# Decays of a selective scan one slot ahead, half of them in SBUF, and images stored once for the depthwise convolutions

## The chip, the cores and the metric

The kernel runs on one core of a Trainium2 chip. The metric is the device time of one execution in microseconds (us); the median of several runs is given. A core has five engines that work side by side, each through its own instructions in order: PE (TensorE, matrix products into PSUM), DVE (VectorE), ACT (ScalarE, activation functions), POOL (GpSimd[...]) and SP (SyncE, which here issues all DMAs). An engine that waits for another holds up everything behind it in its own queue.

## The reference

Four layers act on an image batch x of 4 x 128 x 64 x 64 (float32). The change touches layer 0, whose work is, for each of the four images:

```
x_n  = groupnorm(x)                                   # 32 groups
feat = gelu(depthwise3x3(x_n, conv1_w))
ca   = sigmoid(relu(mean(feat) @ ca1_w.T) @ ca2_w.T)
feat = gelu(depthwise3x3(feat * ca, conv2_w))
score of each pixel from feat and from the variance of x_n over channels
order of the 256 patches of 4 x 4 pixels = argsort(-mean score)
tokens = x_n in that order + pe, layernorm            # 4096 x 128
xm, z  = tokens @ in_proj_w.T                         # 256 + 256 channels
xc     = silu(causal conv1d(xm));  dt, B, C from xc @ x_proj_w.T
h_t = exp(dt_t * A) * h_(t-1) + dt_t * B_t * xc_t     # 256 channels x 16 states
y_t = sum over states of h_t * C_t;   out = ((y + D * xc) * silu(z)) @ out_proj_w.T
x = x + out, put back in the old order of pixels
```

Layer 1 adds a dense 3x3 convolution, layer 2 an attention and a feed-forward part, layer 3 a linear attention and a feed-forward part. They are not touched.

## The kernel before

**Stages.** Layers 0 and 1 are one function, `layers01`. Image 0 is prepared alone ("the opening", `in_order(0)`, to about 280 us). Then `scan` runs over the four images in turn, 8 chunks of 512 tokens each, 32 chunks in all. Beside the scan of image b the preparation of image b + 1 is carried out (`in_order`); beside the last scan, the end of images 2, 0 and 1 (put back, groupnorm, 3x3 convolution). The end of image 3 runs alone.

**The scan.** 16 states times 256 channels are 32 rows of 128 partitions. A chunk has 8 groups g (two states each), a group has four rows q, and a slot handles two of them, so a group takes an even slot (i = 0) and an odd slot (i = 1), and a chunk takes 16 slots. Per group, DVE makes `hs` = dtx * B for all four rows (line 900; B comes from PE in PSUM, `b_ps`, one buffer). Per slot, ACT makes two decays exp(a * dt) of 128 x 512 (line 907) in `psex`, a PSUM pool with two buffers; DVE runs two scans (line 911) with a decay and a row of `hs`; POOL copies the last column into `carry` (line 914) and multiplies both rows by C (line 915). PE sums the products over states into `y_ps`. `hs` has three buffers. C is loaded by SP as a broadcast (`c_sb`, three buffers).

**The order of the work** is written out by hand: inside `manual_schedule` each engine executes in the order of emission. A slot emits, in this order: `hs` (even slots), two decays, `K.flush()` (the delayed work: evacuations, activations and sums that earlier slots put off with `later`), two scans, the two POOL instructions, PE's sums of the group before (odd slots), the loading of C (even slots), one step each of `leave` (the chunk before), `enter` (the next chunk) and the work beside, and at last PE's `b_ps` of the next group (even slots). A decay waits until the scan that used its buffer has run, that is, the scan of the slot before.

**The next chunk.** `enter(n + 1)` makes xc, B, C, dt and dtx of the next chunk on PE, ACT, DVE and POOL; SP copies dt and dtx to both halves of the partitions (`dt2`, `dtx2`, two buffers each). Three of POOL's 128 x 1024 instructions per chunk are from here, a fourth (`yt` * `sz`) from `leave`.

**The depthwise convolutions.** PE takes the taps over ky and 32 channels as contraction: the operand `under` has 96 partitions (3 ky x 32 channels) by 4 groups of channels. SBUF rows of an image are 66 wide with their border. So SP stores the image to DRAM (`image_d`) three times, once for each ky, in two halves, 12 DMAs of 32 partitions each per half (line 443), and for each of 8 pieces of 8 rows `gather` loads 96 x 4 x 528 values in one DMA (line 453, two buffers). `first` and `second` are the convolutions; the stores of the normalized image are emitted when it is filled, the stores of the first result (`fp`) behind its fifth and eighth piece.

**Small parts.** `sort` makes a comparison matrix `before` (line 581) per half of the patches, each time anew. `put_back` makes `perm_inv0/1` in buffers of their own. `Common` makes `same4` and `same16` with their intermediate tiles in a pool that stays.

Of the kernel before, what the change touches and what calls it, by code (L numbers as in the profile page):

```python
# [30 lines left out]
class Common:  # L31
# [3 lines left out]
    def __init__(self, tc, pool):  # L35
        self.slot = 0
        self.late, self.count, self.live, self.held, self.banks = [], 0, set(), set(), 8
        nc = self.nc = tc.nc
        self.tc = tc
        self.pool = pool  # L40

        def const(name, shape, value):
            t = pool.tile(shape, F32, name=name)
            nc.vector.memset(t, value)
            return t

# [21 lines left out]
        self.same4 = self.same_block("same4", 2)  # L68
        self.same16 = self.same_block("same16", 4)
        self.group_mean = pool.tile([P, P], F32, name="group_mean")  # L70
        nc.vector.tensor_scalar(self.group_mean, self.same4, 0.25, None, ALU.mult)

    def shifted(self, name, src, n, ops):

        nc = self.nc
        ti = self.pool.tile([P, n], I32, name=name + "_i")
        nc.vector.tensor_scalar(ti, src, *ops)
        tf = self.pool.tile([P, n], F32, name=name)
# [3 lines left out]
    def same_block(self, name, shift):  # L82
        nc = self.nc
        r = self.shifted(name + "_r", self.row_i, 1, (shift, None, ALU.arith_shift_right))
        c = self.shifted(name + "_c", self.col_i[:, 0:P], P, (shift, None, ALU.arith_shift_right))
        t = self.pool.tile([P, P], F32, name=name)
# [183 lines left out]
def layers01(K, xd, dpool, w, w1):  # L270
# [9 lines left out]
    with ExitStack() as ctx:  # L280
# [44 lines left out]
        image_d = [dpool.tile([4, 96, HW * (HW + 2)], F32, name=f"image_d{i}") for i in range(2)]  # L325
# [52 lines left out]
        ones256 = K.ones[:, 0:1].to_broadcast([P, 256])  # L378

# [43 lines left out]
        def in_order(b, made, work, psum):  # L423
# [13 lines left out]
            def stored(img, i, half):  # L437


                n = HW // 2 * (HW + 2)  # L440
                for g in range(4):
                    for ky in range(3):
                        nc.sync.dma_start(
                            out=image_d[i][g, 32 * ky : 32 * ky + 32, n * half : n * half + n],
                            in_=img[32 * g : 32 * g + 32, HW // 2 * half + ky : HW // 2 * (half + 1) + ky, :].rearrange(
                                "p y x -> p (y x)"
                            ),
                        )

            def gather(i, c):  # L450
                n = 8 * (HW + 2)
                t = unders[c] = work.tile([96, 4, n], F32, name="under", bufs=2)
                nc.sync.dma_start(out=t, in_=image_d[i][:, :, n * c : n * c + n].rearrange("g q f -> q g f"))
# [113 lines left out]
            def sort():  # L567
# [6 lines left out]
                for h in range(2):  # L574
# [5 lines left out]
                    before = small.tile([P, 256], F32, name="before")  # L580
                    nc.vector.scalar_tensor_tensor(before, K.col, K.row[:, h : h + 1], ones256, ALU.is_gt, ALU.mult)
                    eq = small.tile([P, 256], F32, name="eq", tag="rank_eq")
                    nc.vector.scalar_tensor_tensor(eq, sm, cl, before, ALU.is_equal, ALU.mult)
# [137 lines left out]
        def scan(seqs, others, work, psum, psbc, psex, psy):  # L721
# [158 lines left out]

            for _ in enter(0):
                K.flush()
            K.flush()
            bb, cs = spread_b(0, 0), spread_c(0, 0)
            past, leaving, coming = None, iter(()), iter(())
            for n, (b, c) in enumerate(chunks):
# [8 lines left out]
                dt2, dtx2 = entered[n][2:]  # L895
                more = n + 1 < len(chunks)
                coming = enter(n + 1) if more else iter(())
                for g in range(NG):
                    hs = work.tile([P, NQ, CH], F32, name="hs", bufs=3)
                    nc.vector.tensor_tensor(hs, dtx2, bb.unsqueeze(1).to_broadcast([P, NQ, CH]), ALU.mult)  # L900
                    for i in range(2):
                        slot = 2 * g + i
                        two = slice(2 * i, 2 * i + 2)
                        decays = []
                        for q in (2 * i, 2 * i + 1):
                            ex = psex.tile([P, CH], F32, name="decay")
                            nc.scalar.activation(ex, dt2[:, q, :], AF.Exp, scale=a_neg[:, q, g : g + 1])  # L907
                            decays.append(ex)
# [45 lines left out]
        def put_back(xb, om, rank, prep, psum):  # L954
# [4 lines left out]
            for h in range(2):  # L959
                pi = small.tile([P, 256], F32, name=f"perm_inv{h}")  # L960
# [1172 lines left out]
```

## Time and profile before

| | |
|---|---|
| runs, median of 3 | 10019.67 us (10018.24 to 10020.51) |
| profiled execution, its own time | 10014.33 us |
| its span, first to last instruction | 10012.5 us |
| busy in the span: PE, DVE, ACT, POOL | 8755.8, 7222.2, 7414.1, 4804.1 us |
| scan, first to last scan instruction | 280.6 to 2733.4 us |
| busy in it: PE, DVE, ACT, POOL | 2030.9, 2081.3, 1519.5, 1656.2 us |
| scans (line 911), 1024 | 1245.8 us, 1266 ns each |
| decays (line 907), 1024 | 693.0 us, 689 ns each |
| POOL's products (line 915), 512 | 1207.5 us, 2358 ns each |

Lines of the profile name the engine, the operation and output <- inputs, then shapes and how often; in brackets or behind a bar stands the idle time before the instruction and what ended it. In the windows each row gives a stretch in us from the span's start, its length, the busy time of PE, of PE's weight loads, of DVE, ACT and POOL, the share of the PE clock that was granted, the share of the DMA engines and GB/s. A row of the waits says which engine's instruction waited for what: us in total, times, longest. "SPq" is the queue that issues DMAs.

### The profile page before, as it was taken

How to read it: one execution, taken by the hardware profiler on the slowest of the kernel's cores; microseconds unless marked ns; L12 is line 12 of the kernel's file. 1: busy time of each engine (PE TensorE's matmuls, PEld its weight loads, DVE VectorE, ACT ScalarE, POOL GpSimd, SP SyncE). 2: the span in 40 equal slices, each digit the busy share in tenths (PEclk: the TensorE clock that was granted, in tenths of full speed). 3: DMA queues.
4: the chain of work that ended last, by engine and by line, in shares of the span. 5: the costliest groups of instructions: out<-in, count | busy, mean ns of one | idle time of the engine just before them, and what ended most of it. 6: DMA issues, size and time to landing. Idle time of an engine off the chain costs nothing.

```text
span 10012.5 us, 187862 instructions
## 1 busy us (share of the span) xinstructions
PE 8755.8 (87%) x74074; PEld 3353.2 (33%) x74074; DVE 7222.2 (72%) x7883; ACT 7414.1 (74%) x10669; POOL 4804.1 (48%) x3175
## 2 busy tenths in 40 slices
PE   5687888889859999979999979999979999967767
PEld 1122222235433333333333333333333333323433
DVE  1779797998738888848888858888758888743463
ACT  2666766654439999969999969999969999941531
POOL 0567586775525555545555545555545555420000
PEclk9787887889979999989999989999989999978888
DMA  5634536222221211141211141211141111133004
GB/s 127 150 88 101 134 79 152 69 73 81 74 70 37 41 39 39 30 115 38 39 39 39 29 115 39 39 38 39 29 115 39 38 39 39 33 100 118 2 18 152
DMA packets 578291, 669.38 MB, mean 67 GB/s; under 512 B 113592, under 2 KB 369664, under 8 KB 570240
## 3 DMA queue, kind: packets, MB, share of 16 engines
q1 hardware_dynamic: 577408, 657.36, 27.1%
q8 instruction: 584, 9.57, 0.4%
q14 instruction: 299, 2.45, 0.1%
HBM read 446.84 MB, written 143.13 MB: 59 GB/s over the span
## 4 chain that ended last, share of the span: by engine, by line
PE 45%; DVE 4%; DMA 2%; ACT 2%; POOL 1%; issue 1%; SPq 1%; DVEq 0%; POOLq 0%; ACTq 0%
PE ctx_ps L91 20%; PE acc_ps L91 10%; PE score L91 8%; PE ln_xc L91 1%; DMA w<-in_L_ffn_weight 1%; PE ln_var L91 1%; PE hid_ps L91 1%; PE kv L91 1%; PE tok_t L1829 0%; PE ln_var L121 0%; PE pool L91 0%; PE ans_ps L91 0%; DVE ctx L1468 0%; PE o_ps L91 0%; SPq L1210 0%
## 5 line engine op out<-in xcount | busy, mean ns | idle before, releaser
L1534 ACT ACTIVATE ex<-score 128x1024 f32<-128x1024 f32 x5120 | 4927.9, 1037 | 176.0 <-PE score L91 90.2
L91 PE MATMUL ctx_ps<-ex,qt 128*32 128x512 f32 x20480 | 2736.5, 606 | 19.8 <-DVE ctx L1468 19.8
L1483 POOL TENSOR_TENSOR folded<-ex 128x1024 f32<-128x1024 f32 x512 | 1224.2, 2391 | 2124.0 <-ACT ex L1534 1866.1
L1540 DVE STREAM_TRANSPOSE turned<-ex 128x1024 f32<-128x1024 f32 x1536 | 1885.9, 1228 | 351.5 <-ACT ex L1534 279.1
L1516 DVE STREAM_TRANSPOSE turned<-ex 128x1024 f32<-128x1024 f32 x1532 | 1843.0, 1203 | 0.0
L91 PE MATMUL acc_ps<-turned,turned_v 128*32 128x256 f32 x24576 | 1769.4, 379 | 3.0 <-DVE turned L1546 3.0
L911 DVE TENSOR_TENSOR_SCAN hs<-decay,carry,hs 128x512 f32<-128x512 f32 x1024 | 1245.8, 1266 | 248.2 <-ACT decay L907 234.9
L91 PE MATMUL score<-queries,keys 32*128 32x512 f32 x10240 | 1333.6, 497 | 64.4 <-POOL queries L1218 35.8
L91 PEld LDWEIGHTS acc_ps<-turned,turned_v 128*32 128x32 f32 x24576 | 800.8, 110 | 1476.5 <-issue 1327.2
L915 POOL TENSOR_TENSOR hs<-hs,c_sb 128x1024 f32<-128x1024 f32 x512 | 1207.5, 2358 | 108.9 <-DMA c_sb<-c_d 66.5
L907 ACT ACTIVATE decay<-dt,a_neg 128x512 f32<-128x512 f32 x1024 | 693.0, 689 | 662.5 <-DVE hs L911 653.0
L91 PEld LDWEIGHTS score<-queries,keys 32*128 32x128 f32 x10240 | 512.1, 182 | 1160.4 <-ACT ex L1534 801.8
L1346 POOL TENSOR_TENSOR turned_v<-v,quarter 128x1024 f32<-128x1024 f32 x256 | 612.5, 2393 | 266.3 <-PE acc_ps L91 221.8
L91 PE MATMUL y_ps<-hs,pair 128*64 128x512 f32 x2048 | 664.0, 776 | 27.0 <-POOL hs L915 26.9
L1484 POOL TENSOR_TENSOR quarters<-folded 128x512 f32<-128x512 f32 x512 | 658.0, 1285 | 40.1
L91 PEld LDWEIGHTS ctx_ps<-ex,qt 128*32 128x32 f32 x20480 | 406.5, 108 | 655.4 <-issue 599.3
L900 DVE TENSOR_TENSOR hs<-dtx,b_ps 128x2048 f32<-128x2048 f32 x256 | 580.5, 2267 | 55.1 <-PE b_ps L91 29.8
L91 PE MATMUL b_ps<-dbc,state 32*64 32x512 f32 x1024 | 339.6, 745 | 224.5 <-DVE hs L900 224.4
L1534 ACT ACTIVATION_READ_ACCUMULATOR ex<-score 128x1 f32 x2048 | 437.7, 214 | 0.0
L914 POOL COPY carry<-hs 128x2 f32<-128x2 f32 x512 | 98.1, 192 | 700.1 <-DVE hs L911 673.9
L1468 DVE COPY ctx<-ctx_ps 128x512 f32<-128x512 f32 x256 | 176.9, 691 | 329.2 <-PE ctx_ps L91 323.5
L91 PE MATMUL conv<-under,deep 96*32 96x512 f32 x1536 | 217.9, 708 | 136.6 <-DMA under<-image_d 128.3
(371 smaller groups left out, 9156.9 us busy)
## 6 DMA issues: line engine op xcount, KB each, us to landing
c_sb<-c_d SPq DMA_DIRECT2D x512, 128.0 KB
queries<-head_d SPq DMA_DIRECT2D x1024, 64.0 KB
keys<-head_d SPq DMA_DIRECT2D x1024, 64.0 KB
under<-image_d SPq DMA_DIRECT2D x64, 792.0 KB
dt<-dt SPq DMA_DIRECT2D x128, 256.0 KB
dtx<-dtx SPq DMA_DIRECT2D x128, 256.0 KB
v<-value_d SPq DMA_DIRECT2D x1024, 32.0 KB
w<-in_L_ffn_weight SPq DMA_DIRECT2D x32, 1024.0 KB
```

What stands on the lines that cost most here:

```text
L91: self.nc.tensor.matmul(out, lhsT, rhs, start=start, stop=stop)
L900: nc.vector.tensor_tensor(hs, dtx2, bb.unsqueeze(1).to_broadcast([P, NQ, CH]), ALU.mult)
L907: nc.scalar.activation(ex, dt2[:, q, :], AF.Exp, scale=a_neg[:, q, g : g + 1])
L911: nc.vector.tensor_tensor_scan(hs[:, q, :], decays[q - 2 * i], hs[:, q, :], carry[:, g, q : q + 1], ALU.mult, ALU.add)
L915: nc.gpsimd.tensor_tensor(hs[:, two, :], hs[:, two, :], cs.unsqueeze(1).to_broadcast([P, 2, CH]), ALU.mult)
L1346: nc.gpsimd.tensor_tensor(t, v.unsqueeze(2).to_broadcast([P, 4 * BT, 4, HD]), quarter.unsqueeze(1).to_broadcast([P, 4 * BT, 4, HD]), ALU.mult,
L1468: nc.vector.tensor_copy(u, cps)
L1483: nc.gpsimd.tensor_tensor(hs, exs[:, :, 0], exs[:, :, 1], ALU.add)
L1484: nc.gpsimd.tensor_tensor(qs, hs[:, :, 0 : CH // 2], hs[:, :, CH // 2 :], ALU.add)
L1516: nc.vector.transpose(*upright)
L1534: nc.scalar.activation(ex, sps[p], AF.Exp, scale=scale, accum_out=sums[:, t : t + 1] if summed else None)
L1540: nc.vector.transpose(*upright)
```

## The change

- **Decays**: a function `decay(m)` makes the two decays of slot m. The first slot's are made ahead of the loop; each slot then emits the decays of the slot after it, ahead of its own delayed work, and its scans take those made a slot earlier. Those of even slots stay in the two PSUM buffers; those of odd slots go into two SBUF buffers (`decay_b`).
- **Images**: `image_d` has one copy of the image with its border, 128 partitions by 66 x 66. It is stored in four quarters of rows, one DMA each, as soon as the rows are there. `gather` loads a piece with three DMAs, one for each ky, from rows shifted by ky.
- **Small parts**: `before` is made once for each half (`befores`), with an instruction that reads one tensor; `perm_inv0/1` take the buffers of `beats0/1`; the intermediate tiles of `same4` and `same16`, and `same4` itself, go into a pool that is given back.

```
+        with tc.tile_pool(name="temporary", bufs=1) as tmp:
+            self.same4 = self.same_block("same4", 2, tmp, tmp)
+            self.same16 = self.same_block("same16", 4, tmp, pool)
...
-        image_d = [dpool.tile([4, 96, HW * (HW + 2)], F32, name=f"image_d{i}") for i in range(2)]
+        image_d = [dpool.tile([P, (HW + 2) * (HW + 2)], F32, name=f"image_d{i}") for i in range(2)]
...
+        befores = [small.tile([P, 256], F32, name=f"before{h}", bufs=1) for h in range(2)]
+        for h in range(2):
+            nc.vector.tensor_scalar(befores[h], K.col, K.row[:, h : h + 1], None, ALU.is_gt)
...
-            def stored(img, i, half):
-                n = HW // 2 * (HW + 2)
-                for g in range(4):
-                    for ky in range(3):
-                        nc.sync.dma_start(
-                            out=image_d[i][g, 32 * ky : 32 * ky + 32, n * half : n * half + n],
-                            in_=img[32 * g : 32 * g + 32, HW // 2 * half + ky : HW // 2 * (half + 1) + ky, :].rearrange(
-                                "p y x -> p (y x)"
-                            ),
-                        )
+            def stored(img, i, q):
+                lo, hi = 16 * q + 1 if q else 0, 16 * q + 17 if q < 3 else HW + 2
+                nc.sync.dma_start(
+                    out=image_d[i][:, lo * (HW + 2) : hi * (HW + 2)], in_=img[:, lo:hi].rearrange("p y x -> p (y x)")
+                )
             def gather(i, c):
                 n = 8 * (HW + 2)
                 t = unders[c] = work.tile([96, 4, n], F32, name="under", bufs=2)
-                nc.sync.dma_start(out=t, in_=image_d[i][:, :, n * c : n * c + n].rearrange("g q f -> q g f"))
+                for ky in range(3):
+                    at = (8 * c + ky) * (HW + 2)
+                    nc.sync.dma_start(
+                        out=t[32 * ky : 32 * ky + 32],
+                        in_=image_d[i][:, at : at + n].rearrange("(g q) f -> q g f", q=32),
+                    )
...
-                if c == 6:
-                    stored(xp, 0, 0)
+                if c in (3, 5, 7):
+                    stored(xp, 0, c // 2 - 1)
...
-            stored(xp, 0, 1)
+            stored(xp, 0, 3)
             def first_stored(c):
-                if c in (4, 7):
-                    stored(fp, 1, c // 5)
+                if c % 2:
+                    stored(fp, 1, c // 2)
...
-                    before = small.tile([P, 256], F32, name="before")
-                    nc.vector.scalar_tensor_tensor(before, K.col, K.row[:, h : h + 1], ones256, ALU.is_gt, ALU.mult)
-                    nc.vector.scalar_tensor_tensor(eq, sm, cl, before, ALU.is_equal, ALU.mult)
+                    nc.vector.scalar_tensor_tensor(eq, sm, cl, befores[h], ALU.is_equal, ALU.mult)
...
+            def decay(m):
+                n, g, i = m // SLOTS, m % SLOTS // 2, m % 2
+                out = []
+                for q in (2 * i, 2 * i + 1):
+                    ex = work.tile([P, CH], F32, name="decay_b") if i else psex.tile([P, CH], F32, name="decay")
+                    nc.scalar.activation(ex, entered[n][2][:, q, :], AF.Exp, scale=a_neg[:, q, g : g + 1])
+                    out.append(ex)
+                return out
...
+            coming_decays = decay(0)
...
-                        decays = []
-                        for q in (2 * i, 2 * i + 1):
-                            ex = psex.tile([P, CH], F32, name="decay")
-                            nc.scalar.activation(ex, dt2[:, q, :], AF.Exp, scale=a_neg[:, q, g : g + 1])
-                            decays.append(ex)
+                        decays = coming_decays
+                        if slot + 1 < SLOTS or more:
+                            coming_decays = decay(SLOTS * n + slot + 1)
                         K.flush()
...
-                pi = small.tile([P, 256], F32, name=f"perm_inv{h}")
+                pi = small.tile([P, 256], F32, name=f"perm_inv{h}", tag=f"beats{h}")
```

More of the change, by code (lines that the diff above doesn't have):

```diff
@@ L66, in __init__, with shifted, same_block @@
         nc.vector.tensor_scalar(self.row[:, 1:2], self.row[:, 0:1], 128.0, None, ALU.add)
[L68 to L73, printed above, removed]
+        with tc.tile_pool(name="temporary", bufs=1) as tmp:
+            self.same4 = self.same_block("same4", 2, tmp, tmp)
+            self.same16 = self.same_block("same16", 4, tmp, pool)
+            self.group_mean = pool.tile([P, P], F32, name="group_mean")
+            nc.vector.tensor_scalar(self.group_mean, self.same4, 0.25, None, ALU.mult)
+    def shifted(self, name, src, n, ops, pool=None):
         nc = self.nc
-        ti = self.pool.tile([P, n], I32, name=name + "_i")
+        pool = pool or self.pool
+        ti = pool.tile([P, n], I32, name=name + "_i")
         nc.vector.tensor_scalar(ti, src, *ops)
-        tf = self.pool.tile([P, n], F32, name=name)
+        tf = pool.tile([P, n], F32, name=name)
         nc.vector.tensor_copy(tf, ti)
         return tf
-    def same_block(self, name, shift):
+    def same_block(self, name, shift, tmp, pool):
         nc = self.nc
-        r = self.shifted(name + "_r", self.row_i, 1, (shift, None, ALU.arith_shift_right))
-        c = self.shifted(name + "_c", self.col_i[:, 0:P], P, (shift, None, ALU.arith_shift_right))
-        t = self.pool.tile([P, P], F32, name=name)
+        r = self.shifted(name + "_r", self.row_i, 1, (shift, None, ALU.arith_shift_right), tmp)
+        c = self.shifted(name + "_c", self.col_i[:, 0:P], P, (shift, None, ALU.arith_shift_right), tmp)
+        t = pool.tile([P, P], F32, name=name)
         nc.vector.tensor_scalar(t, c, r, None, ALU.is_equal)
@@ L894, in scan @@
                         begin, until, pace = 8, NCH * SLOTS, (NB - 1) * TURNS_END / (NCH * SLOTS - 8)
-                dt2, dtx2 = entered[n][2:]
+                dtx2 = entered[n][3]
                 more = n + 1 < len(chunks)
```

## The prediction

> **What bounds the kernel now.** I read the page first (the 40 slices), then the windows view by chunk of the scan, then the waits of that stretch, then the timeline in three places. The program is the layers in a row; the diff touches layers 0 and 1 only, the first 2880 us of 10012.5, and there two stages: the opening (image 0 prepared alone, to 280 us) and the scan (280 to 2733 us, 32 chunks of 16 slots). Windows of the first eight chunks (from scan to scan; columns are PE, PEld, DVE, ACT, POOL):
>
> ```profile
> 280.60:345.30 64.70, 48.28 (x122) 12.38 (x122) 63.25 (x56) 41.75 (x55) 44.15 (x37) 0.72 0.35 90
> 345.30:419.50 74.20, 56.34 (x192) 14.75 (x196) 59.92 (x45) 48.31 (x64) 52.62 (x43) 0.82 0.87 192
> 419.50:494.50 75.00, 64.17 (x270) 17.19 (x262) 60.14 (x46) 57.19 (x76) 45.20 (x34) 0.82 0.74 173
> 494.50:600.00 105.50, 84.11 (x367) 22.50 (x366) 64.24 (x51) 73.05 (x90) 54.28 (x39) 0.85 0.53 123
> 600.00:687.30 87.30, 70.94 (x222) 20.57 (x226) 78.34 (x71) 51.66 (x79) 61.95 (x49) 0.75 0.28 70
> 687.30:757.60 70.30, 62.67 (x246) 28.20 (x245) 65.34 (x55) 49.95 (x65) 62.66 (x50) 0.93 0.27 64
> 757.60:819.80 62.20, 47.65 (x138) 13.09 (x134) 59.39 (x45) 39.21 (x52) 46.60 (x34) 0.81 0.30 73
> ```
>
> DVE is the bound: 59.4 of 62.2 us in a light chunk. It idles only in the chunks with the two depthwise convolutions (14, 15 and 41 us in the second, third and fourth). The waits of the scan say for whom:
>
> ```profile
> DVE hs L911 <- ACT decay L907: 234.9, 106, 18.1
> PE conv L91 <- DMA under<-image_d: 62.0, 11, 11.4
> ```
>
> That is 78, 69 and 68 us in the first three sequences, 19 in the last (which waits for the 3x3 convolution on PE). The 18.1 us one is at 497: ACT sits in its queue before the Gelu of a convolution whose gathered rows have not landed. So both halves of the change aim at a real loss.
>
> The opening, from the timeline:
>
> ```profile
> 35.45 27.89 SPq L443 DMA_DIRECT2D image_d<-xp  x24
> 63.39 27.61 SPq L453 DMA_DIRECT2D under<-image_d  x6
> 72.37 7.95 PE L91 MATMUL conv<-under,deep 96*32 96x512 f32 x48 [40.63 <-DMA under<-image_d]
> 126.55 13.68 SPq L443 DMA_DIRECT2D image_d<-fp  x12
> ```
>
> The image is complete at 38 us and the first convolution runs at 72: 24 stores and the first gather lie between.
>
> **What the change may collide with.** DVE and POOL around 630 us:
>
> ```profile
> 629.81 2.34 POOL L915 TENSOR_TENSOR hs<-hs,c_sb 128x1024 f32<-128x1024 f32 x1
> 629.92 2.51 DVE L581 SCALAR_TENSOR_TENSOR before<-col,row,ones 128x256 f32<-128x256 f32 x1
> 632.11 1.37 POOL L612 TENSOR_TENSOR pe<-pe,xp 128x512 f32<-128x512 f32 x1
> 632.47 1.29 DVE L583 SCALAR_TENSOR_TENSOR eq<-sm,cl,before 128x256 f32<-128x256 f32 x1
> 633.79 0.48 DVE L585 SCALAR_TENSOR_TENSOR beats<-sm,cl,eq 128x256 f32<-128x256 f32 x1
> ```
>
> A DVE instruction of 0.48 us that reads two tensors in SBUF takes 2.51 beside a POOL product: it ends 0.28 us after the product does. The POOL sum behind it then takes 1.37 (1.17 elsewhere), and the next DVE instruction waits for that one. They take turns, whole instructions at a time, and a DVE instruction already waiting goes ahead of POOL's next. The four scans at 757.57 (4.81 us together), with decays in PSUM, run at full speed across a POOL product.
>
> [...] The old stores are 32 partitions each: 6.49 MB in about 30 us, 217 GB/s; the trace has no store of 128 partitions to compare. [...]
>
> **The change, part by part.**
>
> *Decays one slot ahead.* The same 1024 activations, 0.69 us each on ACT. They wait for the same scans as before (those of the slot before the current one) and stand before the same delayed work, so nothing on ACT moves back; but the scans that need them come a slot later. A lateness of ACT up to one slot (2.4 us of two scans, plus 2.2 for the product in every second slot) is covered. The copies of dt by SP are needed at slot 15 rather than 16; they are issued near slot 10, so at no price. Table loads (155 before L907) alternate as before. Cover gone, a late decay costs what it costs today.
>
> *Half of the decays in SBUF.* In odd slots both inputs of the scans are now in SBUF, 512 scans, and each must have the port to itself. Per pair of slots today: product L900 2.2 + four scans 4.8 = 7.0 on DVE, beside 2 x 2.55 = 5.1 on POOL (carry and product). After: POOL's product of the even slot starts only when the odd scans have ended (its carry, 0.25 us behind the even scans, finds the port taken). From that end POOL needs 2.25 + 0.25 + 2.35 = 4.85; DVE needs 2.2 + 2.4 = 4.6 to reach the next odd scan and waits 0.25; then scan 1.1, carry 0.1, scan 1.1. Period 7.15: the pairs alone cost almost nothing. But the port is now full, so what else POOL does adds up instead of running beside: three sums and products for the next chunk and the gate, 4 x 2.36 alone, 2.2 each on the port, 8.8 per chunk; and DVE's own two SBUF instructions, 1.7. A light chunk: 8 x 7.15 + 8.8 + 1.7 + 0.8 for the rest = 68.5, against 62.2.
>
> So, chunk by chunk (first sequence, before to after): 64.7 to 71 (statistics add 5.4 of DVE, partly beside POOL); 74.2 to 69.5; 75.0 to 70; 105.5 to 86 (PE has 84 us there, some at a low clock, and becomes the bound); 87.3 to 85 (POOL 62 + scans 19 + other DVE pairs 6, less 2 of overlap); 70.3 to 80.5 (twelve more POOL products, L676, 10); 62.2 to 68.5; 63.2 to 69. Sum -3. The other two sequences are 5 us shorter today, mostly in the fourth chunk: +2 each. The last: four chunks bound by PE unchanged, four +4 each, less 11 of decay waits: +5. Scan: +6.
>
> Behind a delayed POOL stand its products, for which PE's y_ps waits in order (up to 2 us later where PE has room); behind a delayed DVE stands PE's b_ps. Neither is late in the chunks that PE bounds.
>
> *Stores and gathers.* 192 stores of 264 KB go, 32 of about 540 KB from 128 partitions come: 2.2 MB instead of 6.5 per image. At the old 217 GB/s 10 us, at the rate of the xb loads (four of 512 KB from 19.6 to about 28 us) below 8; I take 8, beginning at 35. 64 gathers become 192 with the same bytes; in the opening a gather takes 5.7 us from its free buffer to the next convolution. Three pieces of 32 partitions: 0 to 1 us more, I take 0.5. SP issues 224 instead of 256. First convolution at 49 (today 72); pairs of convolutions every 10.4 + 0.5, last at about 95 (today 126, with an 11.7 us wait behind the stores of fp); the second eight at 5.8 us each, set by PE and ACT, end at 146 (today 184). Opening -37, between -28 and -42. In the scan shorter stores also free SP for c_sb; counted in the fourth chunk's gain.
>
> *The rest.* Eight L581 (2.5 us each in the scan) become two at the start; in the fifth chunk's sum. perm_inv in the buffers of beats: their readers ended a sequence ago, no price. Temporaries: none.
>
> Sum: -37 + 6 = -31. On the profiled execution's 10014.3 (span 10012.5 and 1.8 around it) 9983; the median of the runs is 5.3 higher, so 9989, say **9990**.
>
> **Rivals.**
> - *B, the scan isn't held by the port.* Then the middle gaps go and nothing comes: about -10, -10, -19, -7 and -2 per sequence, -140 for three, -10, opening -37: 9833. For it: no scan with two SBUF inputs is in the trace; against it: every other such instruction was held.
> - *C, slower: POOL's product slips between the two odd scans.* POOL then has nothing left during L900 and the even scans: 4.65 + 1.2 + 2.5 + 1.1 = 9.4 per pair of slots, +2.3. In all chunks that PE doesn't bound, about +55 per sequence, +30 in the last, less 37: 10190. It decides early: 14 of 256 pairs eat the -31, and 22 give +20. Against it: at 632.1 the waiting DVE went first.
> - *D, the middle chunks give half.* The port or PE's queue (b_ps, y_ps behind a late product) takes the place of ACT: +17 per sequence: 10040.
> - That the decays don't come ahead can't be: they are emitted there in the fixed order.
>
> **Numbers.** Forecast 0.50 (its own range 9945 to 10040), B 0.08, C 0.17, D 0.25. 0.2%, 20 us, is about what a measurement can tell from no change. Faster: 0.6 of the forecast, B, a tenth of D: 0.41. Same: 0.35 of the forecast, 0.4 of D: 0.27. Slower 0.32. The range leaves out B and most of C: 9890 to 10110.
>
> **What would show it.** Odd slots' scans (decay_b) at 1.5 us or more on average with PSUM ones at 1.2; light chunks near 68 us; POOL's carry and products longer; the wait on decays below 60 us; first convolution near 49 us, scan from about 243. Wrong if odd scans stay at 1.2 (B), or take over 2 (C), or if the fourth chunk stays above 95 (D).

## The result and the profile after

The changed kernel takes **10188.2 us** (10173.0 to 10191.4, 4 runs), beside 10020.1 for the kernel before: a ratio of 1.016, 95% interval 1.0143 to 1.0178. The profiled execution has a span of 10186.1 us, 173.6 above that of before. Its parts:

| | before | after | difference | forecast |
|---|---|---|---|---|
| opening, to the first scan | 280.6 | 230.4 | -50.2 | -37 |
| scan, 32 chunks | 2452.8 | 2657.5 | +204.7 | +6 |
| all that follows, not touched | 7279.1 | 7298.2 | +19.1 | 0 |

So the loss lies in the scan. In what follows, "the port" is a name for what the odd scans and POOL's instructions take in turn, whole instructions at a time. The prediction inferred it from other instructions; for the scans the profile after shows it: each of the 176 odd ones that took over 1.4 us ends 1.04 to 1.09 us after an instruction of POOL has ended, while those with their decay in PSUM took 1.27 us on average beside POOL's instructions of over 1 us and 1.26 away from them. What it is in the hardware, no run shows. Windows of the first chunk and of the fourth to the seventh (the fourth to the sixth stood at 105.5, 87.3 and 70.3 us before):

```profile
230.40:306.00 75.60, 50.45 (x122) 13.13 (x122) 74.44 (x56) 42.06 (x55) 55.05 (x38) 0.69 0.30 85
...
458.60:550.20 91.60, 79.59 (x367) 21.82 (x366) 78.03 (x52) 72.86 (x90) 57.37 (x38) 0.91 0.52 118
550.20:647.80 97.60, 73.76 (x212) 20.62 (x214) 89.69 (x70) 52.87 (x79) 66.38 (x49) 0.71 0.25 63
647.80:738.20 90.40, 71.07 (x254) 30.68 (x252) 82.11 (x55) 50.23 (x65) 72.05 (x50) 0.84 0.20 50
738.20:808.80 70.60, 50.94 (x138) 13.52 (x134) 68.32 (x45) 39.66 (x52) 61.21 (x34) 0.73 0.26 64
```

DVE has about as many instructions as before and is busy for 9 to 17 us more per chunk (65.3 to 82.1 in the sixth); POOL is busier too. Of the first seven only the fourth chunk, where DVE had waited for decays, is shorter. The groups name the instructions that grew, with the two lines of before first:

```profile
L911 DVE TENSOR_TENSOR_SCAN hs<-decay,carry,hs 128x512 f32<-128x512 f32 x1024 | 1245.8, 1266 | 248.2 <-ACT decay L907 234.9 <-ACT dtx L793 0.5
L915 POOL TENSOR_TENSOR hs<-hs,c_sb 128x1024 f32<-128x1024 f32 x512 | 1207.5, 2358 | 108.9 <-DMA c_sb<-c_d 66.5 <-PE conv L91 2.7 <-PE y_ps L91 1.1
...
L923 DVE TENSOR_TENSOR_SCAN hs<-decay_b,carry,hs 128x512 f32<-128x512 f32 x512 | 912.5, 1822 | 7.9 <-ACT decay_b L890 7.9
L923 DVE TENSOR_TENSOR_SCAN hs<-decay,carry,hs 128x512 f32<-128x512 f32 x512 | 628.2, 1268 | 16.6 <-ACT spreads L656 0.5
L927 POOL TENSOR_TENSOR hs<-hs,c_sb 128x1024 f32<-128x1024 f32 x512 | 1349.2, 2635 | 46.4 <-DMA c_sb<-c_d 3.8 <-PE b_ps L93 1.6 <-POOL carry L926 0.6
```

A scan whose decay is in PSUM takes 1268 ns, as before (1266); one whose decay is in SBUF takes 1822, and POOL's products rise from 2358 to 2635. By position in the group: of the 256 first odd scans 52 take over 3 us, of the second 65; the even ones never exceed 1.4. Each scan that was held starts in earnest when some instruction of POOL ends, 1.04 to 1.09 us before its own end. Put down to that instruction, of the 288 us that the odd scans took above 1.26 us each, 207 lie behind POOL's product with C, 72 behind its sums and products for the next chunk (line 132), and 8 behind the rest. The waits, of the scan stage:

```profile
DVE hs L923 <- ACT decay_b L890: 7.9, 6, 2.3
...
DVE hs L914 <- PE b_ps L93: 91.7, 45, 5.7
...
PE y_ps L93 <- POOL hs L927: 89.3, 43, 4.7
```

The wait for decays is gone (234.9 before). In its place DVE waits for `b_ps` (29.8 before), and PE for POOL's products (25 before).

The clock that was granted to PE in the scan fell as well, from 0.84 to 0.80 (the last column but two):

```profile
280.60:2733.40 2452.80, 2030.89 (x7183) 728.20 (x7184) 2081.34 (x1732) 1519.51 (x2037) 1656.16 (x1257) 0.84 0.41 100
...
230.40:2887.90 2657.50, 2118.01 (x7186) 744.95 (x7186) 2401.14 (x1726) 1527.80 (x2035) 1975.91 (x1257) 0.80 0.33 83
```

A slower PE does not explain the loss: DVE's busy time grew by 320 us, more than the scan did, and DVE stood idle for less time, 256 us instead of 371. Whether the clock has a share in the longer waits for `b_ps` is not shown.

### The profile page after: what moved, and what is told of

Read it like the earlier page. It is cut to its first block, busy times and chain, and to the rows that moved or that the text cites. A ratio compares the mean times of both kernels' runs of the same rounds, so it can differ in the third digit from the quotient of the medians.

```text
span 10186.1 us, 187935 instructions
## 1 busy us (share of the span) xinstructions
PE 8846.9 (87%) x74074; PEld 3376.0 (33%) x74074; DVE 7542.1 (74%) x7877; ACT 7420.1 (73%) x10669; POOL 5124.0 (50%) x3175
## 5 line engine op out<-in xcount | busy, mean ns | idle before, releaser
L927 POOL TENSOR_TENSOR hs<-hs,c_sb 128x1024 f32<-128x1024 f32 x512 | 1349.2, 2635 | 46.4 <-DMA c_sb<-c_d 3.8
L923 DVE TENSOR_TENSOR_SCAN hs<-decay_b,carry,hs 128x512 f32<-128x512 f32 x512 | 912.5, 1822 | 7.9 <-ACT decay_b L890 7.9
L93 PE MATMUL y_ps<-hs,pair 128*64 128x512 f32 x2048 | 701.2, 811 | 92.7 <-POOL hs L927 92.0
L890 ACT ACTIVATE decay<-dt,a_neg 128x512 f32<-128x512 f32 x512 | 347.3, 690 | 520.2 <-DVE hs L923 515.1
L914 DVE TENSOR_TENSOR hs<-dtx,b_ps 128x2048 f32<-128x2048 f32 x256 | 580.1, 2266 | 121.9 <-PE b_ps L93 91.7
L923 DVE TENSOR_TENSOR_SCAN hs<-decay,carry,hs 128x512 f32<-128x512 f32 x512 | 628.2, 1268 | 16.6 <-ACT spreads L656 0.5
L93 PE MATMUL b_ps<-dbc,state 32*64 32x512 f32 x1024 | 361.0, 789 | 276.9 <-DVE hs L914 276.8
L890 ACT ACTIVATE decay_b<-dt,a_neg 128x512 f32<-128x512 f32 x512 | 355.8, 718 | 323.8 <-DVE hs L923 315.1
L926 POOL COPY carry<-hs 128x2 f32<-128x2 f32 x512 | 223.8, 437 | 647.5 <-DVE hs L923 621.9
```

What stands on the lines that cost most here:

```text
L93: self.nc.tensor.matmul(out, lhsT, rhs, start=start, stop=stop)
L890: nc.scalar.activation(ex, entered[n][2][:, q, :], AF.Exp, scale=a_neg[:, q, g : g + 1])
L923: nc.vector.tensor_tensor_scan(hs[:, q, :], decays[q - 2 * i], hs[:, q, :], carry[:, g, q : q + 1], ALU.mult, ALU.add)
L926: nc.gpsimd.tensor_copy(carry[:, g, two].unsqueeze(2), hs[:, two, CH - 1 : CH])
L927: nc.gpsimd.tensor_tensor(hs[:, two, :], hs[:, two, :], cs.unsqueeze(1).to_broadcast([P, 2, CH]), ALU.mult)
```

## The experiments

Twelve kernels were run, in four batches with the kernel before in each. Its medians there, and beside the changed kernel, are 10020 to 10031, so less than about 10 us between two batches is not read. In the table, "ratio" is to the kernel before with its 95% interval, and "excess" what the scans with a decay in SBUF took in all above 1.26 us each, from the trace.

| kernel | us | ratio | scan stage us | scans with SBUF decay, ns | excess us |
|---|---|---|---|---|---|
| changed kernel | 10188.2 | 1.016 (1.0143 to 1.0178) | 2657.5 | 1822 | 288 |
| e_images | 9934.3 | 0.9913 (0.9899 to 0.9928) | 2408.4 | none | |
| e_decays | 10273.5 | 1.0253 (1.0236 to 1.027) | 2708.4 | 1829 | 291 |
| e_best | 9924.2 | 0.9898 (0.9883 to 0.9913) | 2410.7 | none | |
| e_own_slot | 10201.6 | 1.0179 (1.0163 to 1.0194) | 2674.3 | 1828 | 291 |
| e_short_best | 9841.6 | 0.9816 (0.9801 to 0.9831) | 2324.6 | none | |
| e_short_after | 9823.8 | 0.9795 (0.9779 to 0.9812) | 2303.2 | 1344 | 43 |
| e_one_product | 10124.5 | 1.0098 (1.0083 to 1.0113) | 2603.2 | 1629 | 189 |
| e_one_of_four | 10077.9 | 1.0048 (1.0031 to 1.0064) | 2552.7 | 2078 | 209 |
| e_even_half | 10084.1 | 1.0054 (1.0039 to 1.0069) | 2558.5 | 1677 | 213 |
| e_short_roots | 10158.2 | 1.013 (1.0115 to 1.0145) | 2648.2 | 1820 | 287 |
| e_flush_after | 10129.2 | 1.0103 (1.0086 to 1.012) | 2600.9 | 1648 | 198 |
| e_flush_best | 9925.7 | 0.9903 (0.9888 to 0.9917) | 2405.4 | none | |

### Which half of the change costs the time

`e_images` is the kernel before with the new stores and gathers alone; `e_decays` is the change without them, small parts included.

```
 e_images, against before
+        image_d = [dpool.tile([P, (HW + 2) * (HW + 2)], F32, name=f"image_d{i}") for i in range(2)]
...
+            def stored(img, i, q):
...
+                for ky in range(3):
...
 e_decays, against the changed kernel: the same lines taken back
```

> The kernel before with the stores and gathers of the change alone; decays as before, all in PSUM. Theory (the shared port of DVE and POOL costs the time, the images pay): opening 50 us shorter as in the changed kernel, waits of the scans on decays down from 235 us to 120 to 160 because the rows land earlier, time 9900 to 9940. Rival (the gathers in three pieces of 32 partitions cost the time): opening shorter but the scan longer than 2453 us, time above 10020.

> The change without its images: stores and gathers as before, decays one slot ahead and half of them in SBUF, small parts as in the change. Theory (port): opening 280 us, the scan about 2660 to 2690, odd scans 1.7 to 1.9 us on average, time 10230 to 10270. Rival (transfers): not slower than before, 10000 to 10030.

Measured: 9934.3 and 10273.5. The images gain 91 us on their own runs of before (10025.6), the decays lose 248; together they lose 157, where the whole change lost 168, so the two hardly touch each other. `e_decays` lies just outside what was expected (10230 to 10270, scan 2660 to 2690). In the profiled executions of `e_images` and of before, 78 us apart, the opening is 47 us shorter and the scan 44; what follows took 13 longer. The wait for decays, in the scan of `e_images`:

```profile
DVE hs L911 <- ACT decay L907: 184.1, 105, 7.2
```

So 51 of the 234.9 us went without any change to a decay, fewer than expected (120 to 160 us were to be left). PE's wait for the gathered rows fell from 62.0 to 11.4 us; ACT held up behind convolutions whose rows were late, as the prediction read it at 497 us, fits this. The fourth chunk falls from 105.5 to 89.1 by the images alone.

### Looking ahead, or the place of the decays

`e_own_slot` is the changed kernel with every decay made in its own slot again, those of odd slots still in SBUF. `e_best` has the change without its decays (all in PSUM, in their own slot) and without the pool for the temporaries of `same4` and `same16`, which are used once at the start.

```
 e_own_slot, against the changed kernel
-                        decays = coming_decays
-                        if slot + 1 < SLOTS or more:
-                            coming_decays = decay(SLOTS * n + slot + 1)
+                        decays = []
+                        for q in (2 * i, 2 * i + 1):
+                            ex = work.tile([P, CH], F32, name="decay_b") if i else psex.tile([P, CH], F32, name="decay")
+                            nc.scalar.activation(ex, dt2[:, q, :], AF.Exp, scale=a_neg[:, q, g : g + 1])
+                            decays.append(ex)
 e_best, against e_own_slot
...
-                            ex = work.tile([P, CH], F32, name="decay_b") if i else psex.tile([P, CH], F32, name="decay")
+                            ex = psex.tile([P, CH], F32, name="decay")
```

> The changed kernel with every decay made in its own slot again, as before; odd slots' decays stay in SBUF. Theory (port): the port's cost stays and the waits on decays come back in part, so at least as slow as the changed kernel: 10190 to 10260, odd scans 1.6 us or more. Rival (making decays ahead delays the other work on ACT and through it PE and DVE): clearly faster than the changed kernel, below 10080.

> The change without its decays: images stored once, the two masks made once, perm_inv in the buffers of beats; all decays in PSUM in their own slot. Theory (port): a little below the images alone, since eight DVE instructions that read two tensors in SBUF go: 5 to 15 us less. Rival: the same within 5 us, since the fifth chunk is bound by something else.

Measured: 10201.6 and 9924.2. Putting the odd decays into SBUF costs 277 us. Making them a slot ahead brings 13 (10201.6 to 10188.2), which the intervals don't tell from nothing. `e_best` is also the version that beats both kernels: 104 us below its own runs of the kernel before (10028.2). It is 10 us below `e_images`, as expected by number, but not for the reason expected: its opening and scan are as long (234.0 and 2410.7 us, against 233.8 and 2408.4), so nothing is seen there of the eight instructions saved.

The account of DVE in the scan stage, `e_best` to the changed kernel, by the durations of its instructions: 1024 scans, 1294.3 to 1581.9, +288; its other instructions apart from `hs`, 314.3 to 350.2, +36; idle, 332.5 to 256.3, -76. That is +248 (the stage grew by 246.7). The idle time that looking ahead could take was small, because of what came next: between `e_own_slot` and the changed kernel the wait for decays goes from 157 to 8, but the wait for `b_ps` from 29 to 92, that for the convolutions from 38 to 49, and that for ACT's part of dt comes to 32.

### Whether POOL's product is the partner

The same two kernels with POOL's product (line 927) cut to 2 of its 512 columns per row, which leaves out nearly all of the multiplication by C; all instructions and waits remain.

```
-                            hs[:, two, :], hs[:, two, :], cs.unsqueeze(1).to_broadcast([P, 2, CH]), ALU.mult
+                            hs[:, two, 0:2], hs[:, two, 0:2], cs[:, 0:2].unsqueeze(1).to_broadcast([P, 2, 2]), ALU.mult
```

> The change without its decays, and POOL's product with C shortened from 512 columns to 2 (the rest of the states isn't multiplied by C): POOL hardly holds the port. Reference for the next run: DVE still bounds the light chunks at about 60 us, time about 20 to 60 us below the same kernel with full products.

> The changed kernel with the same shortened product (the rest of the states isn't multiplied by C). Theory (port): odd scans back at 1.26 us on average or little more, and the decays one slot ahead now gain: 20 to 80 us below the run with shortened products and the old decays. Rival (decays ahead or SBUF itself cost): as slow against that run as the changed kernel is against its like, 150 us or more.

Measured: 9841.6 and 9823.8. The first lies 83 us below `e_best`, more than the 20 to 60 expected, so full products cost the version without SBUF decays something too. With the product all but gone, the change's decays no longer cost 264 us but gain 18, a little less than the 20 to 80 expected. The group of odd scans in `e_short_after`:

```profile
L923 DVE TENSOR_TENSOR_SCAN hs<-decay_b,carry,hs 128x512 f32<-128x512 f32 x512 | 667.7, 1344 | 7.1 <-ACT decay_b L890 7.1
```

1344 ns: a scan with both inputs in SBUF is not slow by itself; it is slow beside POOL's long instructions. Of its 512 scans 23 are still held, all of them behind POOL's other instructions of 128 x 1024, and these hold back 43 us. The wait for decays that looking ahead was to remove is, in `e_short_best`:

```profile
DVE hs L912 <- ACT decay L908: 165.4, 98, 5.8
```

It falls to 7, but DVE's idle time in the scan falls by only 66 us (288 to 222), since it then waits for `b_ps` (25 to 81) and ACT's part of dt (3 to 27). The 43 us of held scans take back most of the 66: the scan is 21 us shorter.

### Where the product gets in

The timeline of the changed kernel shows two patterns. In the first, of a light chunk, the odd scans follow the even ones at once:

```profile
748.78 2.43 DVE L923 TENSOR_TENSOR_SCAN hs<-decay_b,carry,hs 128x512 f32<-128x512 f32 x2
...
748.92 1.09 POOL L926 COPY carry<-hs 128x2 f32<-128x2 f32 x1 [1.21 <-DVE hs L923]
750.09 3.27 POOL L927 TENSOR_TENSOR hs<-hs,c_sb 128x1024 f32<-128x1024 f32 x1
```

This is the pattern of the forecast: the carry finds the port taken (1.09 us for 0.18 of work), and the product waits for the second odd scan (3.27 for 2.36); DVE loses nothing. In the second pattern, of the sixth chunk, something stands between:

```profile
708.25 0.66 DVE L708 COPY perm_s<-perm_t 128x512 f32<-128x512 f32 x1
...
708.39 0.19 POOL L926 COPY carry<-hs 128x2 f32<-128x2 f32 x1 [0.20 <-DVE hs L923]
708.65 2.36 POOL L927 TENSOR_TENSOR hs<-hs,c_sb 128x1024 f32<-128x1024 f32 x1
708.83 6.49 DVE L923 TENSOR_TENSOR_SCAN hs<-decay_b,carry,hs 128x512 f32<-128x512 f32 x2
710.98 3.26 POOL L132 TENSOR_TENSOR dtx<-dt,xc 128x1024 f32<-128x1024 f32 x1
```

A copy out of PSUM, put off by an earlier slot and carried out by `K.flush()` between the even and the odd scans, is not held by POOL: the 24 of the 32 copies of this line that ran beside a long instruction of POOL took 0.67 us on average, the other 8 0.69. During its 0.66 us POOL's carry goes through, and its product, next in line, has the port 0.2 us ahead of the odd scan. That scan waits to the product's end at 711.0; then comes one scan, then POOL's next instruction, which was waiting too, then the second scan: 6.49 us for two scans of 2.4. In 114 of the 256 groups DVE has work between the even and the odd scans; there the odd pair lost 1.74 us on average (198 us in all), in the other 142 groups 0.63 (90 us). The trace also tells which product held a scan. In the 114 groups it is mostly the product of the even slot just before, as in the second pattern (146 us of the 198). In the 142 that product accounts for 0.7 us; there 53 us lie behind the product of the odd slot of the group before, with which POOL is late, and 30 behind the work for the next chunk. Two experiments each take away one side of the meeting in the 114 groups, and a third is the control.

`e_one_product` is the changed kernel with one product of all four rows behind the odd scans, in place of two.

```
-                        nc.gpsimd.tensor_tensor(
-                            hs[:, two, :], hs[:, two, :], cs.unsqueeze(1).to_broadcast([P, 2, CH]), ALU.mult
-                        )
+                        if i == 1:
+                            nc.gpsimd.tensor_tensor(
+                                hs, hs, cs.unsqueeze(1).to_broadcast([P, NQ, CH]), ALU.mult
+                            )
```

> The changed kernel with POOL's two products of a group made as one of 128 x 2048 behind the odd scans. Theory (who gets the port between the two odd scans decides): the odd scans are interrupted less, 1.3 to 1.5 us on average, but PE gets the group later; time 10080 to 10180. Rival (the port is simply full): the sum of holds is the same, time within 30 us of the changed kernel.

`e_flush_after` and `e_flush_best` are the changed kernel and `e_best`, with the delayed work of odd slots emitted behind the odd scans.

```
-                        K.flush()
+                        if i == 0:
+                            K.flush()
                         for q in (2 * i, 2 * i + 1):
                             nc.vector.tensor_tensor_scan(
...
+                        if i == 1:
+                            K.flush()
                         nc.gpsimd.tensor_copy(carry[:, g, two].unsqueeze(2), hs[:, two, CH - 1 : CH])
```

> The changed kernel, but in odd slots the delayed work is emitted behind the odd scans instead of ahead of them, so that on DVE nothing stands between the even and the odd scans; the order on the other engines is the same. Theory T (DVE's short delayed instructions, which need no port, let POOL's carry through, and its product of 2.35 us then takes the port ahead of the odd scans): the 114 groups with DVE work there lose 1.73 us each above the free scans, the 142 without 0.63; with all at 0.63 the scans have 125 us less, of which half to nine tenths reach the end: 10075 to 10125, odd slots' scans 1.6 us or less on average (now 1.82). Rival R (the port is simply full, whatever lies between): what is spared between the scans comes back elsewhere, 10170 to 10200.

> The same move of the delayed work in the kernel without the change's decays (9924): what the move itself is worth where no scan needs the port. Both theories: no more than 20 us either way, 9905 to 9945.

Measured: 10124.5; 10129.2 and 9925.7. With no product due between the scans 64 us of the 264 go; the odd scans stay at 1.63 us, above the 1.3 to 1.5 expected. With the delayed work moved, 59 go (the sixth chunk of the first three sequences falls by about 9 us each), while the same move does nothing without SBUF decays. The excess fell by 89 us, not by the 125 expected, and the time stayed 4 us above the expected range. The trace shows why. The move cleared 71 of the 114 groups, not all: in the other 43 DVE still has work between the even and the odd scans, which does not come by way of that `K.flush()`, such as the statistics of line 171. Those 43 groups lose 1.38 us each, the 213 without such work 0.65, about the 0.63 of before; that makes up the 36 us by which the excess fell short. What the products of a group's own even slot held falls from 147 to 48 us, and what those of the group before held rises from 60 to 94, so a part of the gain comes back at another place.

In both kernels the odd scans still lose 189 to 198 us. In `e_flush_after` 142 of them lie behind products with C; in `e_one_product` these are 71, and 106 lie behind POOL's work for the next chunk. So the work between the scans is a part of the loss, and POOL's lateness another. The group in `e_flush_after`:

```profile
L924 DVE TENSOR_TENSOR_SCAN hs<-decay_b,carry,hs 128x512 f32<-128x512 f32 x512 | 823.2, 1648 | 11.3 <-ACT decay_b L890 11.3
```

### Dose and phase

Both kernels are `e_own_slot` with one condition changed. In `e_one_of_four` the last decay of a group alone is in SBUF; in `e_even_half` those of the even slots are.

```
-                            ex = work.tile([P, CH], F32, name="decay_b") if i else psex.tile([P, CH], F32, name="decay")
+ e_one_of_four              ex = work.tile([P, CH], F32, name="decay_b") if q == 3 else psex.tile([P, CH], F32, name="decay")
+ e_even_half                ex = work.tile([P, CH], F32, name="decay_b") if not i else psex.tile([P, CH], F32, name="decay")
```

> Images as in the changed kernel; each decay made in its own slot; of a group's four decays the last alone is in SBUF, the other three in PSUM. Theory T (what costs is turns between two scans that both need the port, and a full port): one scan in SBUF per group leaves no second one for a product to go before, and the port has slack (4.85 of POOL and 1.2 of DVE in 7.0 us), so the cost is well under half of the 277 us of two in SBUF: 9970 to 10030, light chunks 62 to 66, the one scan 1.5 us at most on average. Rival R (each SBUF scan has its own price, whatever lies beside it): half of 277, so 10063 and light chunks near 66.5.

> As the kernel with the images and SBUF decays in their own slots (10201.6), but the decays of the EVEN slots are in SBUF and those of the odd slots in PSUM. Theory T1 (the port is full, its total decides): 10170 to 10230. Theory T2 (the order of the turns decides: here the hs product of DVE, which needs no port, stands between the odd slot's POOL product and the next SBUF scans, so that each of POOL's two products per group has a stretch of 2.3 us or more of its own, and a carry is no longer caught behind SBUF scans with its product behind it): 10040 to 10140, with scans of the even slots under 1.5 us on average.

Measured: 10077.9 and 10084.1. Half the dose costs 154 us, more than half of 277, so theory T fell: slack of the port over the whole group did not help. Its group says why:

```profile
L914 DVE TENSOR_TENSOR_SCAN hs<-decay_b,carry,hs 128x512 f32<-128x512 f32 x256 | 532.0, 2078 | 0.0
```

2078 ns each, and 193 of 256 over 1.4. In 120 of the 193 POOL starts the even slot's product while the first odd scan runs, with its decay in PSUM (1.27 us on average); the product takes 2.36; so the scan with its decay in SBUF comes in its middle. Over all 256 it waits 0.8 us on average. The rival (a fixed price for each) came within 15 us of the time, but its light chunks (66.5) did not come: they take 71 to 72. And the price is not fixed, as `e_even_half` shows. There as many scans in SBUF as in `e_own_slot` cost 160 instead of 277 us, within the range of T2, though its scans stay above the 1.5 us that T2 named. Its timeline around the copy that did the harm above:

```profile
710.24 0.66 DVE L708 COPY perm_s<-perm_t 128x512 f32<-128x512 f32 x1
...
710.38 0.19 POOL L917 COPY carry<-hs 128x2 f32<-128x2 f32 x1 [2.50 <-DVE hs L914]
710.65 2.35 POOL L918 TENSOR_TENSOR hs<-hs,c_sb 128x1024 f32<-128x1024 f32 x1
710.83 2.44 DVE L914 TENSOR_TENSOR_SCAN hs<-decay,carry,hs 128x512 f32<-128x512 f32 x2
```

The product starts as before, but the odd scans beside it take their decays from PSUM and run at full speed (2.44 us for two). The next product runs beside `hs`, which reads PSUM too and takes 2.25 us there, 2.26 on average. For a single scan, what decided here is not how much of the port the scans use (2078 ns each with one of four in SBUF, 1677 with two) but what POOL has begun when it comes to it. The excess alone doesn't give the time, though: it is 213 us here and 198 in `e_flush_after`, which is 45 us slower. There DVE's idle time and its other instructions are longer by 25 us each.

### A guess that fell

The sixth chunk (70.3 to 90.4 us) was put down to POOL's twelve products there of the normalized tokens (line 679). `e_short_roots` cuts them to one column in 64, which leaves that part of the computation out.

```
-                        nc.gpsimd.tensor_tensor(inner(n, a), inner(n, a), outer(rs, a), ALU.mult)
+                        nc.gpsimd.tensor_tensor(inner(n, a)[:, :, 0:1, 0:1], inner(n, a)[:, :, 0:1, 0:1], outer(rs, a)[:, :, 0:1, 0:1], ALU.mult)
```

> The changed kernel with POOL's sixteen products of the normalized tokens by their inverse deviations (xn by ln_rs) cut to one column in 64, which leaves that part of the computation out. Theory T (POOL's further work costs the time of the port and of what queues behind it): the sixth chunk of the first three sequences falls from 90 to 70 to 74, the fifth by 3 to 6, so 10188 falls by 60 to 75, to 10113 to 10128. Rival R (those chunks are long for another reason, PE's lateness behind the sort and the transposes): they fall by under 8 us each and the time stays above 10155.

Measured: 10158.2. The chunk falls by 3.8 us only, to 86.6, as the rival had it; the scan stage by 9.2. The other 21 us of the 30 lie outside the scan (10 in the opening, which has such products too; 11 behind the scan, where nothing differs). So these products are not what lengthens that chunk. The copies between the scans are a good part of it: `e_flush_after` has it at 81.7.

Another part of that chunk goes by way of PE. From the timeline of the changed kernel:

```profile
666.15 2.34 POOL L838 TENSOR_TENSOR yt<-yt,sz 128x1024 f32<-128x1024 f32 x1
...
668.55 3.78 PE L93 MATMUL out_ps<-yt,out_projT 128*128 128x512 f32 x4 [4.47 <-POOL yt L838]
...
676.35 2.29 DVE L914 TENSOR_TENSOR hs<-dtx,b_ps 128x2048 f32<-128x2048 f32 x1 [4.25 <-PE b_ps L93]
```

POOL is late with `yt`: the carry and the product just ahead of it took 1.17 and 3.27 us, 1.9 more than they take with the port free. PE waits 4.47 us for `yt` with the output projection, with `b_ps` queued behind; and DVE then waits 4.25 us for `b_ps`. How much of the 4.47 the port accounts for is not shown beyond these 1.9.

## Why the prediction was wrong

**The bound and the wait aimed at: right.** DVE bounds the scan, and the wait for decays falls from 234.9 to 7.9 us (below 60 was named).

**"The pairs alone cost almost nothing": this is the step that failed.** Its period of 7.15 us for a pair of slots exists: at 760.56 to 767.67 us it is 7.11. But the working set hs, even scans, odd scans one behind the other, and left out the delayed work that the order of a slot, named in the text before it, puts between. "Its carry, 0.25 us behind the even scans, finds the port taken" holds only without that work, and 114 of the 256 groups have DVE work there; they lost 198 us. Nor does it hold where POOL is late with the product of the group before; the groups without such work lost 90. The odd scans waited 288 us in all, where the forecast had 0.25 us per pair of slots, 64 for the 256.

The time of the first sequence, forecast and measured: 71 and 75.6, 69.5 and 74.4, 70 and 78.2, 86 and 91.6, 85 and 97.6, 80.5 and 90.4, 68.5 and 70.6, 69 and 72.5. The two light chunks at the end, with few copies between scans, are off by 2 to 3.5 us; the fifth and sixth by 10 to 13. That the light ones came near is in part chance: in the seventh chunk odd scans lost 5.2 us behind products with C, where the forecast had 2 (8 times 0.25), and 2.2 behind the work for the next chunk, where it put 8.8. In the last sequence +5 became +46, of which 15 are in the four chunks bound by PE, forecast as unchanged.

**Rival C** gave 10190, 2 us from the result. That closeness is luck: its own terms (+55 three times, +30 and -37), added to the 10019.7 of before, make 10178, and C had every pair at 9.4 us and the odd scans at over 2; they are at 1.82. Its event is real, though. In 65 of the 256 groups a whole instruction of POOL stands between the two odd scans, in 39 of them a product of the kind that rival C named, past the 22 pairs for which it gave a loss of 20 us; in the other 26 it is one for the next chunk. In 52 groups a whole instruction stands ahead of the first odd scan, 43 times the product. The one place from which the forecast read the turns (632.1, where the waiting DVE went first) shows what happened when DVE was already waiting, not who comes first.

**The gain, mis-sized.** The forecast gave the middle chunks' gaps to the decays, and c_sb's share of the fourth chunk to the stores. The images alone took the fourth chunk from 105.5 to 89.1, and 44 us out of the scan. Looking ahead took 66 us of DVE's idle time where the port was nearly free, of the 165 it waited there for decays, since PE's `b_ps` and ACT's part of dt are late next; 18 us of it reached the end. Rival D had named PE's queue for that.

**"Neither is late in the chunks that PE bounds": nearly right there, but nothing was allowed for the other chunks.** In the fourth chunk PE waits for no product of POOL, and DVE 2.6 us for `b_ps`. Over the whole scan PE's waits for POOL's products rose from 25 to 89 us, those for `yt` from 12.5 to 39.8, and DVE's for `b_ps` from 29.8 to 91.7; in the third chunk of the first three sequences DVE waits 7.8, 13.0 and 9.1 us for it, where it waited 0.2 before.

**The opening: right in kind, too small.** -37 became -50 (`e_images`: -47), outside the -28 to -42 given. The first convolution runs at 40.7 instead of 49:

```profile
28.86 3.12 SPq L446 DMA_DIRECT2D image_d<-xp  x4
32.12 17.67 SPq L455 DMA_DIRECT2D under<-image_d  x12
...
40.67 7.80 PE L93 MATMUL conv<-under,deep 96*32 96x512 f32 x48 [23.98 <-DMA under<-image_d]
```

The four stores leave SP from 28.9 on, not from 35, and the first gather follows at 32.

**Open.** The layers behind the scan took 19 us longer, with unchanged work. Over the kernels of this study they took 7277 to 7298 us: 7287 to 7298 with decays in SBUF, 7277 to 7282 without, but 7292 in `e_images`, which has none. The clock granted to PE in that part goes with it: 0.9431 on average before and 0.9413 after, and over the fourteen kernels a lower clock goes with a longer time (correlation -0.87). Why the clock differs there is not shown.

Of the 264 us, moving the flush and merging the products each bring back about 60; they were not run together. That POOL is late with its products in groups without DVE work between the scans is read from the trace; no experiment takes that lateness away alone. Looking ahead with all decays in PSUM was not run, so what it is worth without any scan at the port is not known. That the loss as a whole hangs on POOL's long product is shown by `e_short_after` (an excess of 43 us in place of 288).

## What to carry to other kernels

Moving a DVE operand from PSUM to SBUF can make the instruction take turns with POOL's (the odd scans went from 1266 to 1822 ns): before doing so, list what POOL has in its queue at that moment and how long its instructions are, since here one copy of 0.66 us, which POOL did not hold, was enough to let a product of 2.36 us in first. Place such instructions where POOL's long ones meet them less, as in a group's even slots here (a cost of 160 instead of 277 us), or leave the operand in PSUM. A wait of 235 us is worth only what the next-latest engine leaves of it, so try the cheaper remedy alone first: here the stores brought 91 us, and looking ahead 18 even with POOL's product all but gone.

## What the runs showed of the hardware

- A scan with both inputs in SBUF runs at the same speed as one with its decay in PSUM (1268 ns on average) where POOL does not hold it (minimum 1.18 us and median 1.26 in the changed kernel, 1344 ns on average beside shortened products), and otherwise waits until POOL's instruction has ended, for up to 3.45 us in all: the 176 that took over 1.4 us end 1.04 to 1.09 us after it. POOL's carry and product wait for such a scan in the same way: 1.09 and 3.27 us at 748.92 and 750.09, for 0.18 and 2.36.
- Use of the port below its full share (6.05 of 7.0 us, by the estimate ahead of `e_one_of_four`) gave no safety: one scan in four with both inputs in SBUF still lost 0.8 us each, 2078 against 1267 ns.
- Where both engines had work waiting, from 708.65 to 715.3, they alternated by whole instructions: POOL's product with C (2.36 us), scan, POOL's product for the next chunk (3.26), scan; the two scans took 6.49 us together.
- Exponentials into SBUF took 718 ns on average in the changed kernel, into PSUM 690.
